# A four-layer convolution network on one core: Wu's products on four column tiles, the map's state as a square by ScalarE, layer 3's rows in the image's order

## The chip, the cores and the metric

The kernel runs on one core of a Trainium2 chip. The metric is the device time of one execution in microseconds (us), lower is better. The engines go by the short names of the profile: PE is TensorE (its matmuls), PEld its weight loads, DVE is VectorE, ACT is ScalarE, POOL is GpSimd and SP is SyncE. POOL and SP issue nearly all DMAs of this kernel, each in the order of its own queue.

## The reference

The input x holds 32 images of 8 channels by 256 by 256 pixels in float32. Four layers each add a function of the group-normalised input to their input. Layer 0 is the long one: a coupled map lattice of 15 steps, a small network with 128 hidden channels, and a gate that mixes the two.

```python
def layer0(x, K_local, Wp, bp, Wu, bu, Wg1, bg1, Wg2, bg2):
    grid = drive = x
    for _ in range(15):
        mapped = 3.9 * grid * (1.0 - grid)
        local = conv(mapped, K_local, groups=8)            # 3x3, one kernel a channel
        physics = 0.7 * mapped + 0.3 * local
        grid = 0.85 * physics + 0.15 * drive
    cml = clip(grid, 0.0001, 0.9999)
    h = relu(conv(x, Wp, bp))                              # 8 -> 128 channels, 3x3
    nca = sigmoid(conv(h, Wu, bu))                         # 128 -> 8, 1x1
    gin = concatenate([x, cml, nca], axis=1)
    g = sigmoid(conv(relu(conv(gin, Wg1, bg1)), Wg2, bg2)) # 3x3, then 1x1
    return g * cml + (1.0 - g) * nca

x = x + layer0(gn(x), ...)
x = x + layer1(gn(x), ...)   # 3x3, 8 -> 8, operands rounded to 127 levels
x = x + layer2(gn(x), ...)   # 3x3, 8 -> 8
x = x + layer3(gn(x), ...)   # 5x5 mean, one channel at a time
```

## The kernel before

The kernel has two stages. The first computes layer 0 of all images, the second layers 1 to 3.

**First stage.** Two generators are interleaved in one order that is written out by hand (the scheduler is switched off there). `lattice(b, ahead)` runs the 15 steps of image b, and `gated()`, called the rest below, runs the hidden network and the gate of image b-1. Each `yield` of the lattice hands a number to the rest: the PE time, in us, that the rest may emit before the lattice goes on. After each half-step this is `BLOCK`, 7.4. Each `yield` of the rest gives what it has used: 0.87 for a hidden product, 1.9 for a batch of Wu's products, 2.6 for three gate products. Each half-step also calls `next(ahead)`, one errand: a large DMA, or a piece of the statistics of the next image.

The lattice keeps channels 0 to 5 as patches of 16 by 8 pixels on 128 partitions, 512 patches in the free dimension, in two tiles of three channels each (half 0 and half 1, `states`). The tile holds v(v-1), so that the map and its local sum are one product. A half-step is, for each of three channels, a product inside the patch (`patch_sb`, L368) and one with the neighbours' rim (`ring_sb`, L370) into a PSUM buffer `psc`. There are three such buffers. Then DVE adds the drive (L378), forms v(v-1) in place (L384), and `spread(half)` lets SP issue four DMAs (L246) that copy the rim of the new state to `rings[half]`, for the next step's L370. Channels 6 and 7 live in `strip`, rows of the image, and are convolved by DVE with nine taps a step (L317): three taps in half 0, six in half 1. After the six, DVE clamps the sum (L395), forms v(v-1) into the strip (L396), and `edges()` lets SP issue two DMAs (L250, L251) that copy the strip's edge rows to their neighbours.

The order in half 1 is: products; L378; L384; `spread`; six taps, L395, L396; `edges`. In half 0 it is the same without L395, L396 and `edges`.

In the rest, a product of 72 rows of an im2col tile gives 128 hidden channels of two rows of pixels (`ph`, L606; three buffers), and ACT applies the rectifier (`hh`, L611). Four `hh` are a batch; Wu multiplies each into 32 columns of the PSUM tile `pn` (L582 in `second()`):

```python
for hh, r in four:
    q, i = divmod(r, 4)
    nc.tensor.matmul(pn[32 * q : 32 * q + 32, :], wu_sb[:, i, :], hh,
                     start=i == 0, stop=i == 3)
```

The rows r of a batch are (0, 4, 1, 5) or (2, 6, 3, 7), in the second half plus 8, so q changes between two values within a batch. Sixteen rows of eight channels make the 128 partitions of `pn`. The gate then reads the input (`xq`, from `nr_d`), the lattice's result (`cq`, from `cr_d`) and `nh` with the same order of partitions, 16 products (L508) with their neighbours' rows. The raw input `xc` for the residual comes from `x` by two DMAs a chunk, and DVE adds the result (L533 to L540). `x1_d` takes the image to the second stage. Statistics of an image use the `psc` buffers as well (`stats_parts`).

**Second stage.** For each image `layer1` loads `x1` (L709), rounds it in four pieces on DVE and ACT (`qh`), fetches neighbours' rows (`qb`) and multiplies (L698, L702, bf16). `layer2` does it in float32; its result `x2` goes to DRAM as `x3` in one DMA (L746), and comes back as `y`, with whole rows of the image on partitions, in 16 DMAs (L753). `layer3` normalises `y` into `xr` (L762), copies edge rows (`xr2`, L768), multiplies with a band matrix (L777, L781) and stores from SP. The program writes, in iteration b, layer 3 of image b-3, layer 2 of b-1 and layer 1 of b; there the scheduler decides the order on each engine. `x1`, `x2` and `y` have two buffers each.

Of the kernel before, what the change touches and what calls it, by code (L numbers as in the profile page):

```python
# [18 lines left out]
C = 8  # L19
# [29 lines left out]
BLOCK = 7.4  # L49
# [17 lines left out]
def kernel(  # L67
    ctx, tc, x, patch, ring, taps, pick, wp, bp, wu, bu, wg1, wga, wgb, bg1, wg2, bg2, w1, b1, w2, b2, w3,
# [24 lines left out]
    x3_d = [dram.tile([P, NPX], F32, name=f"x3_d{b}") for b in range(2)]  # L93
# [74 lines left out]
    with ExitStack() as es:  # L168
# [10 lines left out]
        taps_sb = const(wt, taps, [P, 9], "taps_sb")  # L179
        pick_sb = const(wt, pick, [P, P], "pick_sb")  # L180
# [13 lines left out]

        for t in (patch_sb, ring_sb):
            flat = t.rearrange("p c m -> p (c m)")
            nc.vector.tensor_scalar(flat, flat, -R_ * (1.0 - BETA_) * EPS_, None, ALU.mult)
# [3 lines left out]
        )  # L201
        for c in range(CP):
            nc.vector.scalar_tensor_tensor(
                patch_sb[:, c, :], eye_sb, -R_ * (1.0 - BETA_) * (1.0 - EPS_), patch_sb[:, c, :],
                ALU.mult, ALU.add,
            )
# [12 lines left out]
        for t in (*xbs, nh, zero, *hbs, *states, *rings, strip):  # L219
            nc.gpsimd.memset(t, 0.0)  # L220

        xn_d = [dram.tile([C, HP, WP], F32, name=f"xn_d{i}") for i in range(3)]
        nr_d = [dram.tile([P, HB, WP], F32, name=f"nr_d{i}") for i in range(3)]
        cr_d = [dram.tile([P, HB, WP], F32, name=f"cr_d{i}") for i in range(3)]
# [26 lines left out]
        def errands(b):  # L253
# [27 lines left out]
            if b >= 0:  # L281
                for r in four:
                    nc.gpsimd.dma_start(
                        window(
                            nr_d[b % 3], r.start * C * HB * WP,
                            [[WP, P], [C * HB * WP, 4], [1, WP]],
                        ),
                        xbs[b % 2][:, r, :],
                    )
                    yield  # L290
# [3 lines left out]
            for r in range(0, RB, 2):  # L294
                nc.vector.bn_stats(bn[:, r, :], xb[:, r, 1 : 1 + W])
                nc.vector.bn_stats(bn[:, r + 1, :], xb[:, r + 1, 1 : 1 + W])
                yield
# [9 lines left out]
        def lattice(b, ahead):  # L307
# [42 lines left out]
            for c in range(CP):  # L350
                nc.vector.scalar_tensor_tensor(
                    inner(c), dr[:, c], 1.0, dr[:, c], ALU.subtract, ALU.mult
                )
                nc.scalar.mul(dr[:, c], dr[:, c], BETA_)
                if c == 0:
                    nc.scalar.mul(d2, d2, BETA_)
                if c % HALF == HALF - 1:
                    spread(c // HALF)
                yield 1.5
            yield 4  # L360
            for step in range(STEPS):
                for half in range(2):
# [14 lines left out]
                    for c in mine:  # L377
                        nc.vector.scalar_tensor_tensor(  # L378
                            inner(c), pss[c % HALF], FLOOR, dr[:, c], ALU.max, ALU.add
                        )  # L380
                    for c in mine:
                        v = inner(c)
                        if step < STEPS - 1:
                            nc.vector.scalar_tensor_tensor(v, v, 1.0, v, ALU.subtract, ALU.mult)  # L384
                        else:
                            nc.vector.tensor_scalar(
                                dr[:, c], v, 0.0001, 1.0 - 0.0001, ALU.max, ALU.min
                            )
                    if step < STEPS - 1:
                        spread(half)  # L390
# [7 lines left out]
                    if half == 1 and step == STEPS - 1:  # L398
                        nc.vector.tensor_scalar(own, acc, 0.0001, 1.0 - 0.0001, ALU.max, ALU.min)
                    next(ahead, None)  # L400
                    yield BLOCK
# [13 lines left out]
            for r in range(0, RB, 4):  # L415
                nc.gpsimd.dma_start(
                    window(
                        cr_d[b % 3], r * C * HB * WP,
                        [[WP, HB * CP], [C * HB * WP, 4], [1, WP]],
# [5 lines left out]
            for q in range(HB // RQ):  # L425
                for c in range(2):
                    at = (C * RQ * q + CP + c) * row
                    nc.sync.dma_start(
                        window(cr_d[b % 3], at, [[WP, HB], [C * row, RQ], [1, WP]]),
# [26 lines left out]

        place = [0]

        def gated():
# [22 lines left out]
            def gate(n, quarter):  # L482
# [10 lines left out]
                for k in range(2):  # L493
                    nc.gpsimd.dma_start(
                        xc[:, k, :],
                        window(
                            x, b * C * H * W + (k0 + k) * RB * W, [[W, RB], [H * W, C], [1, W]]
                        ),
                    )
# [46 lines left out]
                for _ in stats_parts(ps_c, bn, st, gavr_sb, "psc"):  # L546
# [31 lines left out]
            def second():  # L578
                n, pn, four = late.pop()
                for hh, r in four:  # L580
                    q, i = divmod(r, 4)
# [12 lines left out]
            for n in range(B * NCH):  # L594
# [5 lines left out]
                for half in range(2):  # L600
                    im = ims.pop(0)
                    for rows in ((0, 4, 1, 5), (2, 6, 3, 7)):
                        four = []
                        for i, j in enumerate(rows):
# [11 lines left out]
                            if i == 1 and late:  # L616
                                second()
                                yield 1.9
# [8 lines left out]
            yield 1.9  # L627
# [24 lines left out]
    with ExitStack() as es:  # L652
# [80 lines left out]
        def layer2(b, x2, st):  # L733
# [12 lines left out]
            nc.gpsimd.dma_start(x3, x2)  # L746
# [5 lines left out]
            for k in range(HB):  # L752
                nc.gpsimd.dma_start(  # L753
                    y[RB * (k % 8) : RB * (k % 8) + RB, k // 8, :, :],
                    window(x3, k * W, [[C * NPX, RB], [NPX, C], [1, W]]),
# [48 lines left out]
def laid_out(inputs):  # L804
# [33 lines left out]
    def on_rows(w):  # L838
# [7 lines left out]
        return a.reshape(RB * i, 3, RB * o)  # L846
# [34 lines left out]
    for g in range(4):  # L881
# [6 lines left out]
        taps=np.tile(K[CP:, 0].reshape(2, 9), (P // 2, 1)),  # L888
        pick=np.repeat((np.arange(P) == HB * CP)[:, None], P, 1).astype(f),
# [45 lines left out]
```

## Time and profile before

| | |
|---|---|
| median of three runs | 17,328.34 us (17,284.92 to 17,337.03) |
| profiled execution, its own time | 17,311.55 us |
| its span | 17,309.7 us |
| first stage, one image in | 453 us on the mean of 31 |
| second stage | from about 14,760 us to the end |
| PE busy | 16,500.7 us, 95% of the span |
| DVE busy | 13,265.9 us, 77% |
| ACT busy | 4,089.7 us, 24% |
| POOL busy | 3,931.6 us, 23% |
| mean granted PE clock | 0.964 |

Durations in the profile come from the one profiled execution. A group of instructions is given by its line in the kernel, its engine, what it writes and reads, its shape, and its count; then follow its busy time in us, the mean of one in ns, and the idle time of the engine just before it with what ended that. A float32 product appears as two records of PE. "Windows" give the busy time of each engine in a stretch of time, in the order PE, PEld, DVE, ACT, POOL, then the granted PE clock, the busy share of the DMA engines and GB/s. A timeline line begins with the start and the duration in us.

### The profile page before, as it was taken

Reading aid. Unit: us, or ns where it says so; the run is one execution under the profiler, and the core shown is the slowest. Engines: PE = TensorE matmul, PEld = TensorE weight load, DVE = VectorE, ACT = ScalarE, POOL = GpSimd, SP = SyncE. Lnnn points to the kernel's source line nnn. Section 1 sums busy time; section 2 is a strip of 40 time slices with the busy share of each in tenths; the row PEclk is TensorE's granted clock in tenths of the full one; section 3 lists DMA queues with packets and bytes.
Section 4 is the critical chain, followed back from the end, with each engine's and each line's share of the span. In section 5 each row is a group of like instructions: output and inputs, shape, how many; then the busy total and the mean of one; then the engine's idle time right before and its main releaser. Section 6 shows DMA issues by size and latency. Waiting matters only on the chain.

```text
span 17309.7 us, 133874 instructions
## 1 busy us (share of the span) xinstructions
PE 16500.7 (95%) x42888; PEld 6670.3 (39%) x42888; DVE 13265.9 (77%) x17529; ACT 4089.7 (24%) x5982; POOL 3931.6 (23%) x6517
## 2 busy tenths in 40 slices
PE   5999999999999999999999999999999999899999
PEld 2333333333333333333333333333333333344444
DVE  8788888888888788878888887888888884555554
ACT  0222222222222222222222222222222223111110
POOL 1222222222222222222222222222222223111111
PEclk7999999999999999999999999999999999999999
DMA  3666666666666666666666666666666665455454
GB/s 82 129 129 133 133 131 134 127 132 132 133 132 131 124 133 134 128 128 128 127 134 130 129 132 129 133 133 132 133 130 131 133 127 117 113 129 125 122 131 102
DMA packets 817532, 2208.48 MB, mean 128 GB/s; under 512 B 281741, under 2 KB 485749, under 8 KB 732741
## 3 DMA queue, kind: packets, MB, share of 16 engines
q0 software_dynamic: 464384, 1425.54, 39.8%
q1 hardware_dynamic: 352452, 774.38, 21.6%
q8 instruction: 350, 5.73, 0.2%
q14 instruction: 346, 2.83, 0.1%
HBM read 1078.72 MB, written 404.28 MB: 86 GB/s over the span
## 4 chain that ended last, share of the span: by engine, by line
PE 73%; DVE 18%; DMA 5%; issue 2%; POOL 1%; SPq 1%; ACT 0%; DVEq 0%; POOLq 0%; ACTq 0%
PE ph L606 15%; PE psc L370 12%; PE psc L368 11%; DVE acc L317 10%; PE pg L508 10%; PE pn L582 8%; PE psv L777 6%; PE psv L698 5%; DMA rings<-state 3%; DVE state L384 2%; DVE state L378 2%; PE psv L702 2%; PE psv L781 1%; PE pq L519 1%; DMA im<-xn_d 1%
## 5 line engine op out<-in xcount | busy, mean ns | idle before, releaser
L317 DVE SCALAR_TENSOR_TENSOR acc<-strip,taps_sb,acc 128x1024 f32<-128x1024 f32 x3840 | 4931.3, 1284 | 120.2
L611 ACT ACTIVATE hh<-ph,bp_sb 128x512 f32<-128x512 f32 x4096 | 2812.2, 687 | 8403.9 <-PE ph L606 8338.9
L606 PE MATMUL ph<-im,wp_sb 72*128 72x512 f32 x8192 | 4042.1, 610 | 108.7 <-DMA im<-xn_d 86.6
L378 DVE SCALAR_TENSOR_TENSOR state<-psc,flat 128x512 f32<-128x512 f32 x2880 | 1894.8, 686 | 2072.5 <-PE psc L370 2009.5
L368 PE MATMUL psc<-state,patch_sb 128*128 128x512 f32 x5760 | 2762.9, 614 | 365.9 <-DVE u L112 284.4
L370 PE MATMUL psc<-rings,ring_sb 80*128 80x512 f32 x5760 | 2796.6, 623 | 81.5 <-DMA rings<-state 81.4
L476 POOL DMA_DIRECT2D im<-xn_d x3072 | 1730.5, 568 | 3501.1 <-PE ph L606 3117.7
L606 PEld LDWEIGHTS ph<-im,wp_sb 72*128 72x128 f32 x8192 | 1486.5, 191 | 2223.6 <-issue 2074.8
L582 PE MATMUL pn<-hh,wu_sb 128*32 128x512 f32 x8192 | 2022.0, 616 | 0.0
L368 PEld LDWEIGHTS psc<-state,patch_sb 128*128 128x128 f32 x5760 | 1073.6, 193 | 1921.4 <-issue 1142.3
L370 PEld LDWEIGHTS psc<-rings,ring_sb 80*128 80x128 f32 x5760 | 1138.5, 199 | 1588.6 <-issue 1550.9
L384 DVE SCALAR_TENSOR_TENSOR state<-state 128x512 f32<-128x512 f32 x2688 | 1689.7, 685 | 0.0
L777 PE MATMUL psv<-xr,w_sb 128*128 128x512 f32 x2560 | 1159.7, 595 | 0.5 <-DVE xr L762 0.5
L541 POOL DMA_DIRECT2D x_d<-xc x256 | 152.0, 594 | 4082.8 <-DVE xc L536 4017.9
L582 PEld LDWEIGHTS pn<-hh,wu_sb 128*32 128x32 f32 x8192 | 394.0, 111 | 1469.9 <-issue 1469.9
L508 PE MATMUL pg<-xq,wg_sb 128*128 128x512 f32 x1536 | 734.7, 615 | 13.0 <-DMA xq<-nr_d 13.0
L508 PE MATMUL pg<-cq,wg_sb 128*128 128x512 f32 x1536 | 735.0, 616 | 0.0
L508 PE MATMUL pg<-nh,wg_sb 128*128 128x512 f32 x1536 | 732.8, 614 | 0.0
L698 PE MATMUL psv<-xh,w_sb 128*128 128x512 f32 x1536 | 704.8, 595 | 8.1 <-DVE xh L734 4.1
L452 POOL DMA_DIRECT2D hb<-nh x576 | 320.4, 560 | 1710.4 <-ACT nh L560 1662.8
L777 PEld LDWEIGHTS psv<-xr,w_sb 128*128 128x128 f32 x2560 | 475.7, 189 | 565.9 <-issue 561.5
L786 DVE TENSOR_TENSOR y<-psv,y 128x512 f32<-128x512 f32 x256 | 176.6, 690 | 623.3 <-PE psv L781 623.0
(155 smaller groups left out, 12270.6 us busy)
## 6 DMA issues: line engine op xcount, KB each, us to landing
im<-xn_d POOLq DMA_DIRECT2D x3072, 193.3 KB, 7.3
rings<-state SPq DMA_DIRECT2D x1920, 159.5 KB
rings<-state SPq DMA_DIRECT2D x1920, 106.3 KB
strip<-strip SPq DMA_DIRECT2D x960, 126.0 KB
xn_d<-xb POOLq DMA_DIRECT2D x128, 516.0 KB, 10.3
nr_d<-xb POOLq DMA_DIRECT2D x128, 516.0 KB, 9.0
xq<-nr_d POOLq DMA_DIRECT2D x128, 516.0 KB, 11.6
cq<-cr_d POOLq DMA_DIRECT2D x128, 516.0 KB, 13.7
```

The costliest lines, as they stand in the source:

```text
L317: nc.vector.scalar_tensor_tensor(acc, strip[:, dy : dy + RQ, dx : dx + W], taps_sb[:, 3 * dy + dx : 3 * dy + dx + 1], d2 if dy == 1 and dx ...
L368: nc.tensor.matmul(pss[-1], patch_sb[:, c, :], inner(c), start=True, stop=False)
L370: nc.tensor.matmul(pss[c % HALF], ring_sb[:, c, :], rings[half][:, c % HALF, 0 : TX * SY].rearrange("p (x y) -> p x y", y=SY)[:, :, 0:TY], ...
L378: nc.vector.scalar_tensor_tensor(inner(c), pss[c % HALF], FLOOR, dr[:, c], ALU.max, ALU.add)
L384: nc.vector.scalar_tensor_tensor(v, v, 1.0, v, ALU.subtract, ALU.mult)
L476: nc.gpsimd.dma_start(im[24 * dy : 24 * dy + 24, k, 0:run], window(xn_d[b % 3], at, [[HP * WP, C], [1, 3], [1, run]]),)
L508: nc.tensor.matmul(o, wg1_sb[:, s, dx, :], src[:, :, dx : dx + W], start=s == dx == 0, stop=False,)
L582: nc.tensor.matmul(pn[32 * q : 32 * q + 32, :], wu_sb[:, i, :], hh, start=i == 0, stop=i == 3,)
L606: nc.tensor.matmul(ph.rearrange("p (k w) -> p k w", w=W), wp_sb, im[:, :, j * WP : j * WP + W], start=True, stop=True,)
L611: nc.scalar.activation(hh, ph, AF.Relu, bias=bp_sb)
L698: nc.tensor.matmul(o, w[:, dx, :], src[:, 2 * i : 2 * i + 2, dx : dx + W], start=dx == 0, stop=False,)
L777: nc.tensor.matmul(o, w3_sb[:, dx, :], xr[:, k, 2 * g : 2 * g + 2, dx : dx + W], start=dx == 0, stop=False,)
```

## The change

**Wu and the numbering of rows.** In `second()` q and i change places, and a batch takes rows (0, 1, 2, 3) or (4, 5, 6, 7), so that its four products go to four different column groups of 32. Row r of a block of 16 then stands at position (r mod 4) · 4 + r div 4. Weights are permuted to match, `nr_d` and `cr_d` are written in that order, and the raw input is written once to a new DRAM tensor `xr_d` in that order (four more errands' DMAs an image), from where `xc` comes in one DMA a chunk. The estimate for a batch in the `yield` is 1.05 instead of 1.9, and `BLOCK` is 6.5.

**The state as a square.** The tile now holds (v - 1/2)², which is v(v-1) + 1/4. The constant goes into the drive (`lift`), and the rim's border is 1/4 instead of 0. L378 writes its sum back to PSUM, and ACT forms the square from PSUM into the state. ACT also forms the first state and drive of an image.

**The order in a half-step.** It is now: products; the sum; taps, and in half 1 L395, L396 and `edges`; 1.7 us of the rest; squares; `spread`. `held` keeps the statistics of the gated image out of the PSUM buffers meanwhile.

**Layer 3's rows.** `x3_d` has the image's own order. It is written in 16 DMAs, one for each of the 16 positions, and `y` is read in two.

```diff
-BLOCK = 7.4
+BLOCK = 6.5
...
-    x3_d = [dram.tile([P, NPX], F32, name=f"x3_d{b}") for b in range(2)]
+    x3_d = [dram.tile([C, H, W], F32, name=f"x3_d{b}") for b in range(2)]
...
+        lift = wt.tile([P, CP], F32, name="lift")
+        nc.vector.tensor_reduce(lift, kern_sb, AX.X, ALU.add)
+        nc.vector.tensor_scalar(
+            lift, lift, 0.25 * R_ * (1.0 - BETA_) * EPS_, 0.25 * R_ * (1.0 - BETA_) * (1.0 - EPS_),
+            ALU.mult, ALU.add,
+        )
+        minus = wt.tile([P, 1], F32, name="minus")
+        nc.vector.memset(minus, -0.5)
...
                 nc.vector.bn_stats(bn[:, r + 1, :], xb[:, r + 1, 1 : 1 + W])
+                if r < 8:
+                    nc.gpsimd.dma_start(
+                        window(
+                            xr_d[(b + 1) % 3], r // 2 * C * HB * W,
+                            [[W, P], [4 * C * HB * W, 4], [1, W]],
+                        ),
+                        xb[:, 2 * r : 2 * r + 4, 1 : 1 + W],
+                    )
                 yield
...
             for c in range(CP):
-                nc.vector.scalar_tensor_tensor(
-                    inner(c), dr[:, c], 1.0, dr[:, c], ALU.subtract, ALU.mult
-                )
-                nc.scalar.mul(dr[:, c], dr[:, c], BETA_)
+                nc.scalar.activation(inner(c), dr[:, c], AF.Square, bias=minus)
+                nc.scalar.activation(
+                    dr[:, c], dr[:, c], AF.Identity, bias=lift[:, c : c + 1], scale=BETA_
+                )
...
                     for c in mine:
-                        nc.vector.scalar_tensor_tensor(
-                            inner(c), pss[c % HALF], FLOOR, dr[:, c], ALU.max, ALU.add
-                        )
-                    for c in mine:
-                        v = inner(c)
-                        if step < STEPS - 1:
-                            nc.vector.scalar_tensor_tensor(v, v, 1.0, v, ALU.subtract, ALU.mult)
-                        else:
+                        ps = pss[c % HALF]
+                        nc.vector.scalar_tensor_tensor(ps, ps, FLOOR, dr[:, c], ALU.max, ALU.add)
+                    if step == STEPS - 1:
+                        for c in mine:
                             nc.vector.tensor_scalar(
-                                dr[:, c], v, 0.0001, 1.0 - 0.0001, ALU.max, ALU.min
+                                dr[:, c], pss[c % HALF], 0.0001, 1.0 - 0.0001, ALU.max, ALU.min
                             )
-                    if step < STEPS - 1:
-                        spread(half)
                     for dy in (1,) if half == 0 else (0, 2):
...
                         edges()
...
+                    held.append(half)
+                    yield 1.7
+                    if step < STEPS - 1:
+                        for c in mine:
+                            nc.scalar.activation(inner(c), pss[c % HALF], AF.Square, bias=minus)
+                        spread(half)
+                    held.clear()
                     next(ahead, None)
-                    yield BLOCK
+                    yield BLOCK - 1.7
...
-                for k in range(2):
-                    nc.gpsimd.dma_start(
-                        xc[:, k, :],
-                        window(
-                            x, b * C * H * W + (k0 + k) * RB * W, [[W, RB], [H * W, C], [1, W]]
-                        ),
-                    )
+                nc.gpsimd.dma_start(xc, xr_d[b % 3][:, k0 : k0 + 2, :])
...
-                    q, i = divmod(r, 4)
+                    i, q = divmod(r, 4)
...
-                    for rows in ((0, 4, 1, 5), (2, 6, 3, 7)):
+                    for rows in ((0, 1, 2, 3), (4, 5, 6, 7)):
...
-                                yield 1.9
+                                yield 1.05
...
-            nc.gpsimd.dma_start(x3, x2)
+            for r in range(RB):
+                m = r % 4 * 4 + r // 4
+                nc.gpsimd.dma_start(
+                    window(x3, r * W, [[H * W, C], [RB * W, HB], [1, W]]),
+                    x2[C * m : C * m + C, :].rearrange("p (k w) -> p k w", w=W),
+                )
...
-            for k in range(HB):
+            for k in range(2):
                 nc.gpsimd.dma_start(
-                    y[RB * (k % 8) : RB * (k % 8) + RB, k // 8, :, :],
-                    window(x3, k * W, [[C * NPX, RB], [NPX, C], [1, W]]),
+                    y[:, k, :, :], window(x3, k * P * W, [[W, P], [H * W, C], [1, W]])
                 )
```

## The prediction

> **What bounds the kernel now.** I read the page's sums and slices first, then the groups, then the timeline of one image, then the DMA queues' waits. TensorE (PE) is busy 95% of the span, in nearly every slice.
>
> ```profile
> PE 16500.7 (95%) x42888; PEld 6670.3 (39%) x42888; DVE 13265.9 (77%) x17529; ACT 4089.7 (24%) x5982; POOL 3931.6 (23%) x6517
> ...
> PE   5999999999999999999999999999999999899999
> ```
>
> There are two stages. To about 14,760 us the lattice of image b runs beside the gated network of image b-1, one image in 453 us; then layers 1 to 3 take 2,550 us, some 78 us an image. In both PE is the bound: the windows give it 435.9 us of 453 in an image of the first stage and 499.9 of 500 in the second.
>
> ```profile
> 15500.00:16000.00 500.00, 499.85 (x1324) 222.52 (x1322) 292.37 (x582) 67.86 (x97) 77.89 (x123) 1.00 0.51 124
> 6358.00:6811.00 453.00, 435.89 (x1151) 173.70 (x1150) 371.04 (x462) 118.67 (x174) 109.84 (x185) 0.98 0.66 133
> ```
>
> The groups show what is edited: Wu's products (L582) and VectorE's (DVE's) product v(v-1) (L384).
>
> ```profile
> L582 PE MATMUL pn<-hh,wu_sb 128*32 128x512 f32 x8192 | 2022.0, 616 | 0.0
> ...
> L384 DVE SCALAR_TENSOR_TENSOR state<-state 128x512 f32<-128x512 f32 x2688 | 1689.7, 685 | 0.0
> ```
>
> In the timeline one batch of Wu's products lasts from 6002.76 to the next matmul at 6004.60: 1.84 us for eight records. They start in pairs, 6 ns apart, so two column tiles already run together.
>
> ```profile
> 6002.76 1.91 PE L582 MATMUL pn<-hh,wu_sb 128*32 128x512 f32 x8
> ...
> 6004.60 1.99 PE L606 MATMUL ph<-im,wp_sb 72*128 72x512 f32 x4
> ```
>
> The lattice is a chain beside this. For a half-step starting at 6371.75 (half 1) the ring products start at 6374.4; DVE then works through L378, L384, six taps, L395 and L396:
>
> ```profile
> 6377.88 1.89 DVE L384 SCALAR_TENSOR_TENSOR state<-state 128x512 f32<-128x512 f32 x3
> 6379.69 7.88 DVE L317 SCALAR_TENSOR_TENSOR acc<-strip,taps_sb,acc 128x1024 f32<-128x1024 f32 x6
> 6387.60 0.69 DVE L395 TENSOR_SCALAR acc<-acc 128x1024 f32<-128x1024 f32 x1
> 6388.33 1.23 DVE L396 SCALAR_TENSOR_TENSOR strip<-acc 128x1024 f32<-128x1024 f32 x1
> ```
>
> SyncE's (SP's) queue issues the ring copies (L246) right after L384, and the strip's two edge copies (L250, L251) only after L396. At L250 it stands on DVE some 8 us each time; nothing urgent is behind it.
>
> ```profile
> SPq L250 <- DVE df L533: 1050.3, 122, 13.0
> SPq L250 <- DVE bn L296: 932.1, 124, 7.6
> SPq L250 <- DVE state L378: 737.4, 104, 8.1
> ```
>
> I followed the 80 packets of 6,804 bytes of each ring copy: from its first issue to its last packet it takes 8.1 us when GpSimd's (POOL's) large copies are absent, up to 15.5 us beside them, 10.3 us on the mean. It lands a median 9.6 us (half 0) or 11.3 us (half 1) before PE wants it. So PE sets the step: two half-steps take 25.7 us outside the two places per image where a statistics product holds a PSUM buffer (PE idle 4.2 and 5.0 us, then half clock for 3.4 and 10.2 us: some 20 us an image).
>
> **What the Trainium skill says.** "TensorEngine Tiling (Array Packing)", Tiling Modes, lists 128×32 as four tiles that work in parallel, and says that a change of mode drains the engine: the trace agrees for two tiles (0.43 us a pair, 0.19 us lost round the batch). "TensorE: Matmul & The Clock Gate", Part 3, measured 3.07 times for four row tiles and says that column tiles come close; no run here shows four. "DMA: Bandwidth & Descriptors", Anatomy of one DMA: a semaphore wait happens on the issuing sequencer, not in the DMA engines; the L250 waits agree. "VectorE: DVE Perf Modes", the errata table: a ScalarE (ACT) pass of 512 out of PSUM is (172+512)/1.2 GHz = 570 ns; the trace has 687 (L611), which I use.
>
> **The change part by part.**
>
> Wu on four tiles: before, 0.10 + 1.84 = 1.94 us a batch. Four at once need two slots of 0.43 plus the same 0.19: 1.05 us (by 3.07 times, 4 × 0.856 / 3.07 = 1.12; if they do not run together, 1.94). I take 1.05: 0.89 × 32 batches = 28 us of PE an image, 910 us in all, if PE still sets the step.
>
> The square on ACT: DVE loses 84 L384 and six L351 an image at 0.685, 62 us of 371. ACT gains 90 passes at 0.687, 62 us on 119; it idles most of the time, so the work is covered. DVE's L378 now writes PSUM, which no row shows: 0.63 to 0.80 us against 0.686 (fastest and slowest PSUM-reading rows of this size, with margin); I take 0.69. The three PSUM buffers are now held until ACT's squares, which stand in ACT's in-order queue after 1.7 us of gated work: about 4.5 us after the products instead of 0.8. Behind them wait ACT's rectifiers; PE has three buffers for those, so a late DVE can stop PE for 1 to 2 us. Statistics products now also wait for the squares.
>
> The moved ring copies decide. All four copies of half 1 now follow the edge copies in SP's queue; they used to precede them. Their first issue after the ring products' start r is: L378 done at r + 3.5, six taps and L395, L396 to r + 13.3 (L384's 1.9 us is gone), two edge issues 1.65 us, so r + 15.0. Before, it was r + 5.4. The square is ready at about r + 7.5, so the wait is all the strip's. Then the copy: half 1's durations by step before were 8.1, 12.9, 11.4, 15.5, 8.7, 12.3, 9.4, 13.3, 9.4, 8.1, 14.6, 8.1, 8.4, 8.2 us, mean 10.6; the edges' 252 packets just ahead of it add some 0.7, less crossing into half 0's kinder places (mean 10.0): 10.3 + 0.7. With 0.3 us to start PE: 15.0 + 11.0 + 0.3 = 26.3 us a step. PE alone would need 25.7 - 2 × 0.9 = 23.9. So the ring's wait takes the place of Wu's 0.9 us: 14 × (26.3 - 25.7) = +8 us an image. Of the statistics stalls about half (10 us) hides in the ring's wait. ACT does the twelve first passes alone, +2. Sum: 0 us an image, between -28 (copies at 8.1 us, all of Wu's gain kept) and +15 (long copies, each wait over 3.4 us halving the clock; late DVE behind the seven gate operations of 4.8 us).
>
> Rows through xr_d: 128 POOL issues of 512 KB at 0.80 us more, 256 of xc at 0.56 fewer: -41 us on an engine busy 110 of 453. The 64 MB written are 3% more traffic, already in the upper end. Constants and the new small sums at the start: a few us. The renumbered rows themselves: 0, the same products on permuted weights.
>
> Layer 3's rows: x3 goes out in 16 issues an image instead of one, y comes in two instead of 16. Count is 18 against 17, so I would call it hidden; but the planner's order of POOL's queue changes too. Before, for each image: x3 out, y in, then x1 of three images on, a period early:
>
> ```profile
> 15983.29 0.56 POOL L746 DMA_DIRECT2D x_d<-x  x1 [55.17 <-DVE x L743]
> 15990.15 5.45 POOL L753 DMA_DIRECT2D y<-x_d  x10 [6.30 <-DMA x_d<-x]
> ...
> 16003.20 1.86 POOL L709 DMA_DIRECT2D x<-x_d  x1 [0.76 <-DMA y<-x_d]
> ```
>
> In the built program POOL's queue repeats over three images: x3(2) first row, y(1), x3(2) other rows, then x1(3), y(2), x1(4), x1(5), x3(3), x3(4) first row, y(3) and so on, while PE runs layer 2 of image 2, then layer 1 of image 3, then layer 3 of image 1. So x1(3) is asked for only when layer 2 of image 2 has ended, and PE wants it at once. In us after that end: x3's first row at 1.3; y(1), 2 MB, at the 131 GB/s of the present y copies (262 KB in 2 us) to 18; the other x3 rows at a like rate to 28 to 33; x1(3) in 7 to 13, so 36 to 44; four quantized pieces (DVE 0.80 + 0.75 + 0.68 each, ACT 1.06) 10; the neighbours' copy 4; the last products 4. Layer 1 ends at 54 to 62 instead of 7: I take 50 lost. For y(3), asked for after layer 2 of image 4 and wanted 7 us later: 18 us to land, normalising 4.4, edge copy 3 to 9, less 4.3 of products: I take 14. Ten rounds: 10 × 64 = 640 us; ends 10 × 45 and 10 × 80.
>
> **Sum.** 17,311.6 (the profiled execution; span 17,309.7) + 0 + 640 = 17,952; the median of the runs stands 17 higher: 17,970.
>
> **The rivals.** (a) Ring copies land fast and PE stays the bound in the first stage: -28.4 × 31 = -880; with layer 1's loss 17,090: faster. It decides where the copy takes under 8.6 us on the mean (15.0 + 8.6 + 0.3 = 23.9). For it: 8.1 us in seven of 14 places or close; against: POOL's copies do not go away. (b) Layers 1 to 3 lose nothing (x1 in time) and the first stage is even: 17,330. Against: PE's and POOL's orders are fixed in the program. (c) The waits add up: +15 an image, 18,440. (d) The four tiles do not run together: PE needs 25.7 again beside a chain of 26.3, and stalls hide less: +10 an image, 18,280.
>
> **How the numbers follow.** Forecast 0.50; (a) 0.13; (b) 0.06; (c) and (d) 0.31. About 0.3% is what a measurement of this kernel can tell from no change. Faster 0.15 (a, a part of b), same 0.04, slower 0.81. The range leaves out the deep end of (a) and of (c): 17,250 to 18,450.
>
> **What would show it.** Wu's batch at 1.05 us; PE waiting on the ring copies in half 1, several us; SP's L265 waiting on DVE, the copies behind it; PE under 90% busy in both stages; POOL's x3 copies waiting, then PE idle some 50 us every third image. Wrong if PE stays above 95% in either stage, or an image takes under 435 us.

## The result, and the profile after

| | before | after |
|---|---|---|
| median | 17,328.15 us | 19,224.97 us |
| runs | 17,284.92 to 17,337.03 (4) | 19,200.07 to 19,257.56 (4) |
| first stage, to layer 1's first product | 14,780 us | 15,939 us |
| second stage, from there to the last product's end | 2,524 us | 3,253 us |
| one image of the first stage, mean of 29 | 453.1 us | 488.8 us |

The ratio is 1.110, 95% interval 1.108 to 1.113: the change makes the kernel 11.0% slower. The forecast was 3.7% slower, 17,970 us, and the result lies above its range. Of the 1,888 us between the two profiled spans, 1,160 came in the first stage, where I had put nothing, and 729 in the second, where I had put 640.

The page of the changed kernel, its sums, then the slices of PE and of the granted clock: PE falls to 7 and 8 tenths only in the last seven slices, the second stage, while its clock is at 7 or 8 tenths in the first 32.

```profile
PE 17131.2 (89%) x42888; PEld 6886.5 (36%) x42888; DVE 11684.7 (61%) x14652; ACT 5772.1 (30%) x8862; POOL 3928.5 (20%) x6421
...
PE   5899999999999999999999999999999997787878
...
PEclk7888888888888888888888888888888898898989
```

Windows of the changed kernel, one image of the first stage and 500 us of the second (columns as for the kernel before). Before, PE stood still for 17 of 453 us and had clock 0.98; now for 40 of 489, at 0.88. In the second stage it had no idle time at clock 1.00, and now 103 us of 500.

```profile
6358.00:6847.00 489.00, 448.50 (x1129) 177.24 (x1128) 318.61 (x370) 170.43 (x263) 109.15 (x181) 0.88 0.59 125
16400.00:16900.00 500.00, 396.59 (x999) 173.28 (x998) 223.25 (x425) 51.27 (x71) 59.17 (x91) 0.88 0.41 98
```

The groups of the changed kernel: the edit of the operations did what it should. DVE's sum into PSUM (L402) takes 697 ns, the square is ACT's (L421), Wu's group (L606) is down from 2,022 us. But the ring products (L393) waited 688 us on their copies, against 81 us before (L370).

```profile
L402 DVE SCALAR_TENSOR_TENSOR psc<-psc,flat 128x512 f32<-128x512 f32 x2880 | 1957.5, 697 | 5140.3 <-PE psc L393 5131.2
...
L393 PE MATMUL psc<-rings,ring_sb 80*128 80x512 f32 x5760 | 3055.4, 671 | 819.6 <-DMA rings<-state 687.8
...
L421 ACT ACTIVATE state<-psc,minus 128x512 f32<-128x512 f32 x2688 | 1697.9, 689 | 2678.6 <-DVE psc L402 2661.9
...
L606 PE MATMUL pn<-hh,wu_sb 128*32 128x512 f32 x8192 | 1257.6, 687 | 0.0
```

**One wait, step by step.** The timeline of PE in the changed kernel, around a step of half 1. Counts are records, two for each product. Wu's batch runs from 6444.47 to the next product at 6445.47: 1.00 us, so four tiles do run together. The ring products start at 6452.44, those of the next step at 6482.00, after 7.33 us of waiting for the copy.

```profile
6444.47 1.06 PE L606 MATMUL pn<-hh,wu_sb 128*32 128x512 f32 x8
6445.47 1.99 PE L630 MATMUL ph<-im,wp_sb 72*128 72x512 f32 x4
...
6452.44 2.74 PE L393 MATMUL psc<-rings,ring_sb 80*128 80x512 f32 x6
...
6482.00 3.75 PE L393 MATMUL psc<-rings,ring_sb 80*128 80x512 f32 x4 [7.33 <-DMA rings<-state]
```

The same stretch on SP's queue: the edges go out at 6465.79, once DVE's L413 is done, and half 1's four ring copies only from 6467.58, 15.1 us after their step's start, though ACT had their squares ready by 6456.7. Half 0's four follow at once, in the same line of eight.

```profile
6465.79 0.83 SPq L265 DMA_DIRECT2D strip<-strip  x1
6466.66 0.80 SPq L266 DMA_DIRECT2D strip<-strip  x1
6467.58 13.35 SPq L261 DMA_DIRECT2D rings<-state  x8
```

**The clock after it.** PE's timeline goes on without a hole, and every product takes twice its time, up to 6504 or so: 5.46 us for six records of ring products that took 2.74, 3.62 for four of hidden products that took 1.88. Only when six records of full height come in a row (L391, 128 rows) does the speed return: L393 is back at 2.74.

```profile
6482.00 5.46 PE L393 MATMUL psc<-rings,ring_sb 80*128 80x512 f32 x6 [7.33 <-DMA rings<-state]
6487.26 1.92 PE L630 MATMUL ph<-im,wp_sb 72*128 72x512 f32 x2
6488.96 1.91 PE L532 MATMUL pg<-ha,wga_sb 96*128 96x512 f32 x2
6490.67 1.91 PE L533 MATMUL pg<-hb,wgb_sb 72*128 72x512 f32 x2
6492.38 3.62 PE L630 MATMUL ph<-im,wp_sb 72*128 72x512 f32 x4
6495.93 1.94 PE L606 MATMUL pn<-hh,wu_sb 128*32 128x512 f32 x8
6497.79 3.78 PE L630 MATMUL ph<-im,wp_sb 72*128 72x512 f32 x4
6501.37 4.20 PE L391 MATMUL psc<-state,patch_sb 128*128 128x512 f32 x6
6505.40 2.74 PE L393 MATMUL psc<-rings,ring_sb 80*128 80x512 f32 x6
```

The Trainium skill, "TensorE: Matmul & The Clock Gate", Part 1, says that the full clock comes after at least one busy window of about 3.4 us. Here PE is busy for over 20 us before it does, so busy time alone is not what counts. The mean spell at half clock lasts 14.9 us (206 of them from 1,000 to 13,500 us of the span); before, 7.2 us (115): there are more spells, and the mean one is twice as long.

**What brings the clock back.** The traces of before, after, a1, c1, c2, e1 and f1 (below) show it. Every change of the clock in them falls on a grid of 3.41 us. I took each such window of the first stage, from 1,000 to 13,500 us, and weighted PE's time in it by the rows of its products (rows of zeros counted in), as a share of 128. Of the 3,230 windows at half clock, none of the 1,736 with a share under 0.74 was followed by full clock, and all of the 895 with 0.86 or more were; the 599 between them went either way. At full clock, all 994 windows under 0.40 were followed by half clock, and none of the 20,714 with 0.55 or more. Busy time alone does not sort them: in the changed kernel PE was busy through 810 windows at half clock, and after 606 of these the clock stayed at half. In the stretch above, the window from 6494.07 to 6497.48 holds hidden products and most of a batch of Wu, 98 of 128 rows on the mean (0.76), and the clock stays at half; the one from 6500.90 to 6504.31, mostly L391, has 120 rows (0.94), and full clock follows.

**The sum of an image.** From the records of PE and of the clock, the mean of 29 images (the first two and the last left out). "Cold" is time in which PE works at half clock; half of it is lost. (The expectations below count all time at half clock, 118 us in the changed kernel, of which PE works in 111.5.) The work at full speed is what is left of the image after the idle time and half the cold time.

| kernel | image | PE idle | cold | work at full speed |
|---|---|---|---|---|
| before | 453.1 | 16.8 | 26.8 | 423.0 |
| after | 488.8 | 36.4 | 111.5 | 396.6 |
| a1_spread_first | 446.2 | 22.8 | 54.2 | 396.3 |
| c1_full_rows | 464.8 | 50.1 | 33.2 | 398.1 |
| e1_two_tiles | 467.5 | 21.6 | 44.1 | 423.8 |
| f1_block | 487.4 | 43.4 | 95.3 | 396.4 |
| c2_before_full | 444.9 | 17.0 | 10.1 | 422.9 |
| a9_best_block | 441.6 | 35.1 | 21.0 | 396.0 |
| a10_sp | 427.5 | 22.9 | 16.2 | 396.4 |

The last column is a check on this way of counting: it takes two values only, 423 with Wu on two column tiles and 396 to 398 on four. So the change took 26.4 us of work from an image, and added 19.6 of idle time and 42.3 by the clock: +35.5.

**The second stage.** POOL's timeline in the changed kernel, from the end of layer 2 of an image: first row of x3, then y of the image before, then the other rows of x3 (the last at 17,079), and only then layer 1's x1 (L733).

```profile
17059.51 0.59 POOL L772 DMA_DIRECT2D x_d<-x  x1 [75.10 <-DVE x L767]
17060.30 1.84 POOL L782 DMA_DIRECT2D y<-x_d  x2 [0.20 <-issue]
17062.13 3.58 POOL L772 DMA_DIRECT2D x_d<-x  x6
...
17079.11 0.59 POOL L772 DMA_DIRECT2D x_d<-x  x1 [0.34 <-DMA x_d<-x]
17081.71 0.58 POOL L733 DMA_DIRECT2D x<-x_d  x1 [2.01 <-DMA x_d<-x]
```

And PE in the same stretch: it waits 33.73 us for the first rounded piece, which x1 holds up, and 8.03 us for the neighbours' copy.

```profile
17098.33 5.54 PE L722 MATMUL psv<-qh,w_bf 128*128 128x512 bf16 x15 [33.73 <-ACT qh L702]
17111.90 2.31 PE L726 MATMUL psv<-qb,w_bf 72*128 72x512 bf16 x5 [8.03 <-DMA qb<-qh]
```

### The profile page after: what moved, and what is told of

Same layout as the page of the kernel before. It is cut to its first block, busy times and chain, and to the rows that moved or that the text cites. A ratio compares the mean times of both kernels' runs of the same rounds, so it can differ in the third digit from the quotient of the medians.

```text
span 19198.3 us, 136492 instructions
## 1 busy us (share of the span) xinstructions
PE 17131.2 (89%) x42888; PEld 6886.5 (36%) x42888; DVE 11684.7 (61%) x14652; ACT 5772.1 (30%) x8862; POOL 3928.5 (20%) x6421
## 5 line engine op out<-in xcount | busy, mean ns | idle before, releaser
L402 DVE SCALAR_TENSOR_TENSOR psc<-psc,flat 128x512 f32<-128x512 f32 x2880 | 1957.5, 697 | 5140.3 <-PE psc L393 5131.2
L630 PE MATMUL ph<-im,wp_sb 72*128 72x512 f32 x8192 | 4661.8, 690 | 232.8 <-DMA im<-xn_d 119.3
L393 PE MATMUL psc<-rings,ring_sb 80*128 80x512 f32 x5760 | 3055.4, 671 | 819.6 <-DMA rings<-state 687.8
L391 PE MATMUL psc<-state,patch_sb 128*128 128x512 f32 x5760 | 2879.7, 637 | 174.8 <-DVE u L112 86.1
L630 PEld LDWEIGHTS ph<-im,wp_sb 72*128 72x128 f32 x8192 | 1663.5, 215 | 2737.3 <-issue 2164.7
L421 ACT ACTIVATE state<-psc,minus 128x512 f32<-128x512 f32 x2688 | 1697.9, 689 | 2678.6 <-DVE psc L402 2661.9
L393 PEld LDWEIGHTS psc<-rings,ring_sb 80*128 80x128 f32 x5760 | 1184.5, 210 | 2466.7 <-issue 2461.6
L391 PEld LDWEIGHTS psc<-state,patch_sb 128*128 128x128 f32 x5760 | 1139.2, 203 | 1860.5 <-issue 1390.2
L606 PE MATMUL pn<-hh,wu_sb 128*32 128x512 f32 x8192 | 1257.6, 687 | 0.0
L772 POOL DMA_DIRECT2D x_d<-x x512 | 318.8, 632 | 2357.6 <-DVE x L767 2108.8
L527 PE MATMUL pg<-cq,wg_sb 128*128 128x512 f32 x1536 | 785.4, 652 | 0.0
```

The lines of the kernel that those rows point to most:

```text
L391: nc.tensor.matmul(pss[-1], patch_sb[:, c, :], inner(c), start=True, stop=False)
L393: nc.tensor.matmul(pss[c % HALF], ring_sb[:, c, :], rings[half][:, c % HALF, 0 : TX * SY].rearrange("p (x y) -> p x y", y=SY)[:, :, 0:TY], ...
L402: nc.vector.scalar_tensor_tensor(ps, ps, FLOOR, dr[:, c], ALU.max, ALU.add)
L421: nc.scalar.activation(inner(c), pss[c % HALF], AF.Square, bias=minus)
L527: nc.tensor.matmul(o, wg1_sb[:, s, dx, :], src[:, :, dx : dx + W], start=s == dx == 0, stop=False,)
L630: nc.tensor.matmul(ph.rearrange("p (k w) -> p k w", w=W), wp_sb, im[:, :, j * WP : j * WP + W], start=True, stop=True,)
```

## The experiments

Every ratio is to the kernel before on the same chip. Labels that begin with a, e and f, and c1, start from the changed kernel; b4 and c2 start from the kernel before.

**The place of the ring copies: a1_spread_first.** Half 1's edges are issued after its ring copies.

```diff
-                        edges()
...
                         spread(half)
+                        if half == 1:
+                            edges()
```

> One part of the change undone: the strip's two edge copies are issued after half 1's ring copies again, everything else as in the changed kernel (19,225 us). Theory A, the ring copies behind the edges make PE wait and let its clock fall: PE's idle time ahead of the ring products falls from 24 us an image to under 5, the half clock from 118 us an image to 30 to 60, the image from 489 us to 425 to 440, so 17,100 to 17,750 us in all; layers 1 to 3 stay as slow as they are. Rival B, the squares on ACT and the PSUM buffers held for them are what slows the lattice: the image stays over 470 us, over 18,600 us in all. Rival C, PE's clock falls because Wu's products on four tiles leave too little activity: half clock stays near 118 us an image though the waits go, 18,200 to 18,700 us.

17,772.29 us, ratio 1.026 (1.024 to 1.028): 1,453 us back, all in the first stage. PE's group of ring products in this kernel waits for copies as little as before:

```profile
L393 PE MATMUL psc<-rings,ring_sb 80*128 80x512 f32 x5760 | 2816.8, 627 | 125.7 <-DMA rings<-state 76.4 <-issue 30.4 <-DMA strip<-strip 18.8
```

So the order in SP's queue makes the waits: idle time falls by 13.6 us an image and cold time by 57. With that order alone put back, the image is 7 us under that of before. The total lies just over its range, and the image is 446 us, not 425 to 440; the cold time that is left, 54 us, is twice that of before. Rival B is out.

**Layer 3's copies: a2_rows_back and a3_both.** x3 keeps the layout of before; because of the new row numbers it is written by four DMAs of 32 partitions, and y is read by 16 again. a3 is this together with a1's edit.

```diff
-            for r in range(RB):
...
+            for j in range(4):
+                nc.gpsimd.dma_start(
+                    window(x3, j * C * NPX, [[4 * C * NPX, 4], [NPX, C], [1, NPX]]),
+                    x2[32 * j : 32 * j + 32, :],
+                )
```

> Layer 3's rows as before, as far as the new numbering allows: x3 goes out in four DMAs of 32 partitions and y comes in 16, and with them the order in which POOL's queue holds the x1 loads comes back to one a period ahead. The first stage is as in the changed kernel. Theory D, the late x1 and y are what layers 1 to 3 lose: that stage falls from 3,259 us to 2,520 to 2,560, so 18,470 to 18,560 us in all. Rival E, the second stage is slow for the DMAs' own traffic in short rows, not the order: little comes back, 18,900 us or more.

> Both undone together: edge copies after half 1's ring copies, and layer 3's rows as before; Wu on four tiles, the square on ACT and the renumbered rows stay. Theories A and D add up: 16,400 to 17,000 us, faster than both kernels, with PE over 94% busy in the first stage. If Rival B or C holds, 17,500 us or more.

a2: 18,946.78 us, ratio 1.094 (1.092 to 1.096). a3: 17,461.99 us, 1.009 (1.006 to 1.012). Only 292 and 283 us of the 729 came back: the second stage took 2,961 and 2,970 us, against 2,524 before. Both missed: theory D had the second stage back at 2,520 to 2,560 us. What still kept it long was open.

**Rows in use and the clock: c1_full_rows and c2_before_full.** The 72-row and 80-row products get 128 rows; the added weights are zero, and `im_all` are two tiles of 128 rows, zeroed once. c1 does it to the changed kernel, c2 to the kernel before.

```diff
-        rings = [wt.tile([RING, HALF, SN], F32, name=f"rings{i}") for i in range(2)]
+        rings = [wt.tile([P, HALF, SN], F32, name=f"rings{i}") for i in range(2)]
...
-                im = imp.tile([72, 2, 8 * WP], F32, name="im")
+                im = im_all[half]
```

> The changed kernel, with the products of 72 rows (the hidden ones) and of 80 rows (the ring's) taken over all 128 rows: the added rows of weights are zero, those of the moving tile zero or 1/4, so nothing else changes and each product streams the same 512 columns. The trace of the changed kernel shows the clock staying at half for a median of 13.7 us once it has fallen (6.8 before the change), through windows filled with these products and with Wu's, and rising after windows with products of 128 rows. Theory F, rows in use count for the clock: half clock falls from 118 us an image to under 70, the image from 489 us to 450 to 470, 18,000 to 18,700 us in all. Rival G, the clock goes by PE's idle time alone, or zero rows count for nothing: 19,150 to 19,300 us, half clock as it was.

> The kernel before, unchanged but for its 72-row products of the input (Wp) and 80-row products of the ring, which are padded to 128 rows with zero weights: the same number of products of the same length. Theory F (the clock follows the rows in use as well as the time in use): half-clock time in the first stage falls from 29.8 us per image to 8 to 20 us, worth 5 to 11 us per image, total 16,950 to 17,200 us. Theory G (only holes in the product stream count): 29.8 us stay, total 17,280 to 17,370 us. A loss (17,400 us or more) would mean that the padding costs TensorE or DMA time in itself.

c1: 18,467.43 us, ratio 1.066 (1.064 to 1.068). PE is idle for longer, 50.1 us an image, yet cold for 33 instead of 111: with as many holes and more, the clock came back sooner. c2: 17,058.83 us, 0.985 (0.982 to 0.987), cold time 10 instead of 27. So rows in use count for the clock, in either kernel, and the zero rows cost at most 1.5 us of work an image.

**Tiles or block: e1_two_tiles and f1_block.** f1 changes `BLOCK` alone, the first pair of lines below; e1 also puts Wu back on two tiles, with its `yield` of 1.9.

```diff
-BLOCK = 6.5
+BLOCK = 7.4
...
-                    for rows in ((0, 1, 2, 3), (4, 5, 6, 7)):
+                    for rows in ((0, 1, 4, 5), (2, 3, 6, 7)):
```

> The changed kernel with Wu's products on two column tiles again (row numbering, square, spread order and layer 3 as changed; the budget of a block back at 7.4 and Wu's share at 1.9). It puts back some 0.85 us of TensorE work per batch, 28 us per image, outside the lattice as before. Theory P (the Wu saving was real and merely buried under the ring waits; the clock does not care how Wu is tiled): 28 us x 31 images come on top, half-clock time stays at 105 to 130 us per image, total 19,950 to 20,150 us. Theory T (with four tiles the clock stays low longer because a window of Wu and 72-row products no longer holds enough work in the array; two tiles let it come back): half-clock time per image falls from 118 to 50 to 85 us and gives back 15 to 30 us per image, total 19,150 to 19,600 us. Theory A (only the ring chain counts, TensorE work is hidden in its waits): TensorE idle per image falls from 36 to below 15 us, total 19,200 to 19,350 us. The second stage stays at 3,260 us in all three.

> The changed kernel with one number put back: the budget of other TensorE work in a block, 7.4 as before instead of 6.5; Wu stays on four tiles. The run with two tiles had both put back and gained 697 us although it does 28 us more TensorE work per image. Theory K (that gain was the block's: with 0.9 us less cover per half the ring copies arrive too late, waits come and the clock falls): TensorE idle falls from 36 to 18 to 25 us per image and half-clock time from 118 to 40 to 65 us as with two tiles, but without their 28 us, total 17,600 to 18,000 us. Theory T (it was the tiles: two tiles keep more work in the array and the clock comes back sooner): idle 30 us or more, half-clock time 95 us or more, total 18,900 to 19,300 us. Between them both count. The second stage stays at 3,260 us.

e1: 18,528.54 us, ratio 1.069 (1.066 to 1.072), quicker than the changed kernel although it does 27 us more work an image, and quicker than any of its theories had it (19,150 us at the least). f1: 19,157.32 us, 1.106 (1.102 to 1.109), as its theory T. The windows of ten images each show it, the changed kernel, then e1, then f1, each line from its own kernel (second number PE busy, then the clock third from the end):

```profile
6436.65:11324.16 4887.51, 4529.92 (x11382) 1793.70 (x11381) 3195.30 (x3710) 1703.20 (x2630) 1096.26 (x1811) 0.88 0.59 125
```

```profile
6166.03:10820.38 4654.35, 4455.70 (x11381) 1751.62 (x11380) 3203.86 (x3710) 1711.60 (x2630) 1093.45 (x1810) 0.95 0.61 132
```

```profile
6398.97:11277.11 4878.14, 4445.00 (x11381) 1781.66 (x11380) 3202.35 (x3710) 1699.99 (x2630) 1092.06 (x1810) 0.88 0.59 126
```

The longer block halves the waits on ring copies (from 23.9 to 12.5 us an image) and yet leaves clock 0.88; the two tiles bring 0.95. But the pair does not differ in the tiles' effect on the clock alone: with four tiles the longer block runs the rest dry, so that PE's idle time as a whole is 43.4 us in f1 against 21.6 in e1, and there are 9.3 spells at half clock an image against 5.8. The spells are shorter too, 7.9 us against 12.0.

Their length follows from the windows. At half clock a batch of Wu takes 1.87 us on four tiles and 3.56 us on two (medians). A window that holds a whole batch on four tiles, and hidden products else, has by these medians (1.87 × 128 + 1.54 × 72) / 3.41 = 103 of 128 rows, a share of 0.80, in the range that goes either way; on two tiles the batch alone is longer than a window. So four tiles save PE's time and take full-height work out of the stretch in which the clock could recover.

**What was left in the second stage: b4_writes.** One line of the kernel before: four writes of x3 in place of one.

```diff
-            nc.gpsimd.dma_start(x3, x2)
+            for j in range(4):
+                nc.gpsimd.dma_start(x3[32 * j : 32 * j + 32, :], x2[32 * j : 32 * j + 32, :])
```

> The kernel before, unchanged but for one line of layer 2: x3 is written by four DMAs of 32 partitions instead of one of 128, the same bytes to the same places. Theory R (the rest of the second stage's loss lies in GpSimd's order: with four writes the planner puts the next image's x1 load ahead of y's sixteen reads, y lands later, and layer 3's first products wait): the second stage grows from 2,524 us to 2,930 to 3,000 us as in the changed kernel with the rows' copies put back, the first stage stays, total 17,720 to 17,830 us. Rival (four writes are as good as one, and what is left comes from the rows numbered anew): 17,290 to 17,380 us.

17,790.29 us, ratio 1.026 (1.024 to 1.028), second stage 2,984 us: the number of writes makes the whole rest of a2 and a3. POOL's timeline in this kernel shows the order that the planner now makes, x1's load (L709) ahead of y's reads and behind a wait of 9.85 us for its buffer:

```profile
16538.85 1.98 POOL L747 DMA_DIRECT2D x_d<-x  x4 [60.40 <-DVE x L743]
16550.68 0.56 POOL L709 DMA_DIRECT2D x<-x_d  x1 [9.85 <-DVE x L727]
16551.41 4.98 POOL L754 DMA_DIRECT2D y<-x_d  x7 [0.17 <-issue]
```

y's last read is issued 33 us after x3's first write on the mean; in the kernel before, where x1's load comes after y, 19 us. That this order on POOL is what costs the time is not shown, for the planner's order changed on other engines as well. DVE first normalises y (L763) a median of 82 us after x3's first write, although y has landed after 44; before, 34 and 27. And PE, idle for 308 us of this stage (before, 42; the clock costs another 178), waits mainly for DVE's statistics (L101, 88 us; L108, 65) and for the edge copies of `xr` (102), not for y itself.

**Putting it together: a6_best, a8_best, a9_best_block, a10_sp.** a6 is a3 with full rows and with x1 loaded by SP. a8 is a6 with layers 1 to 3 on the row order of before: x1 is loaded in four quarters, by POOL, x3 written in one DMA, and the weights of layers 1 and 2 are not permuted. a9 is a8 with `BLOCK` 7.4. a10 is a8 with the quarters issued by SP, as the lines below have it.

```diff
-            nc.gpsimd.dma_start(x1, x1_d[b])
+            for j in range(4):
+                nc.sync.dma_start(
+                    x1[32 * j : 32 * j + 32, :],
+                    window(x1_d[b], j * C * NPX, [[4 * C * NPX, 4], [NPX, C], [1, NPX]]),
+                )
```

> The kernel with half 1's ring copies ahead of the edge copies and layer 3's rows in four writes and sixteen reads, with two things more: the 72-row and 80-row products padded to 128 rows with zero weights, and layer 1's load of x1 issued by SyncE instead of GpSimd, so that no load of x1 stands ahead of y's reads on GpSimd's queue. Theory R (what was left of the second stage's loss, 437 us, is y's reads waiting behind x1's load): the second stage falls from 2,976 us to 2,520 to 2,650 us. Theory S (it is the order that the planner gives TensorE and VectorE around layer 3): it stays at 2,850 us or more. First stage: theory F of the clock, half-clock time 55 us per image to 20 to 35 us, image 445.6 to 428 to 437 us; if rows don't count there, 445. Totals: F and R 16,500 to 16,850 us, under the kernel before; F and S 16,900 to 17,200 us.

> The fastest kernel so far with layers 1 to 3 on the rows in the order of before: x1's load puts the rows back in order (four loads of 32 partitions on GpSimd in place of one), and x3 is written by one DMA as before. First stage as there, 426.8 us per image. Theory R (the second stage's loss is the planner's order of GpSimd's copies: y behind x1): x3 is ahead of y again with at most one quarter of x1 between them, the second stage falls from 2,710 us to 2,520 to 2,590 us, total 16,430 to 16,520 us. Theory Q (more and smaller copies of one queue cost in themselves, wherever they stand): 2,650 us or more, total 16,560 us or more.

> The same kernel as the one with layers 1 to 3 on the rows of before, and the block's budget 7.4 instead of 6.5. If the ring copies still come late at 6.5 with their new place ahead of the edges (waits on them are only 2.7 us per image there), 7.4 brings at most 3 us per image: total 16,340 to 16,500 us, like its twin or up to 0.5% faster. If cover beyond the need only delays the lattice (blocks last 0.9 us longer and the work left for between the images doesn't shrink by as much), up to 4 us per image more: up to 16,650 us.

> The kernel with layers 1 to 3 on the rows of before (x1's load in four quarters), these quarters issued by SyncE instead of GpSimd: GpSimd has only x3's write and y's reads, as early as before, and the quarters are spread over the image between SyncE's small copies. Theory R: the second stage falls from 2,838 us (quarters on GpSimd, the last one behind y's reads) to 2,520 to 2,620 us, total 16,480 to 16,590 us. Rival (the quarters behind SyncE's edge copies come late as well, or hold these up): 2,710 us or more, 16,670 us or more.

| kernel | median | ratio | second stage |
|---|---|---|---|
| a6_best | 16,619.34 us | 0.959 (0.957 to 0.961) | 2,710 us |
| a8_best | 16,804.94 us | 0.969 (0.968 to 0.971) | 2,838 us |
| a9_best_block | 17,259.66 us | 0.995 (0.994 to 0.997) | 2,844 us |
| a10_sp | 16,494.11 us | 0.951 (0.950 to 0.953) | 2,546 us |

a6 got its first stage and missed the second. x1's load is gone from POOL's queue, and yet y's first read is issued 12.8 us after x3's first write, as in b4 (12.6; before, 7.3): with four writes y is late wherever x1's load stands. Still the second stage is 260 us shorter than in a3; the planner's orders changed again, and which of them brought this is open. a8 missed too: in 29 of 32 images a quarter of x1 stands between x3's write and y's first read, and PE waits 182 us in all for layer 1's neighbours (10 us of it at 15,338). Its time lies in its rival's range; neither run tells whether the number of copies in one queue has a cost of its own. a9 lies far over its range: the longer block ran the rest dry, and PE waits 10.0 us an image for the transposes' input and 8.5 for `xq`, where a8 has 0.8 and 2.6. In a10, which differs from a8 only in the queue of the quarters, POOL's timeline is that of the kernel before again, y straight behind x3:

```profile
15547.32 0.57 POOL L777 DMA_DIRECT2D x_d<-x  x1 [58.51 <-DVE x L774]
15554.20 6.05 POOL L784 DMA_DIRECT2D y<-x_d  x11 [6.31 <-DMA x_d<-x]
```

a10 beats both kernels, by 4.9% and by 14%: it keeps the four tiles, the square and `xr_d`, and loses neither the copies' places nor the clock.

## Why the prediction was wrong

- **Sign and places: right, but for one sign.** Slower, ring copies behind the edges, x1 behind x3: all seen. PE under 90% came in the second stage alone (79% in the window shown). In an image of the first stage PE is busy for 452 of 488.8 us, 93%: what it loses there is mostly the clock, not idle time.
- **Wu on four tiles: right.** A batch was put at 1.05 us and took 1.00; an image was to lose 28 us of work and lost 26.4. Rival (d) is out.
- **The square and DVE's sum: right.** 689 and 697 ns against 687 and 690. The statistics stalls hid as supposed: before the patch products PE waited 9.2 us an image for them and now 2.8.
- **The ring chain: the path was right, its sum 2 us short.** From half 1's step to the next a median of 28.8 us passed, where 26.3 was put (26.4 before). The first issue came a median of 15.2 us after the step's start, as put, and the copies took 9.6 us on the mean, 11.0 put; but from the last packet to a waiting PE it took a median of 2.0 us, not 0.3. PE waited for the copy in 164 of 406 steps; in the others it came to these products later than the copy. That PE's idle time grew by 19.6 us, where 14 × 2.4 - 10 = 24 was put, is luck in part: fewer waits, but longer ones. Rival (a) leaned on seven copies of 14 near 8.1 us; its list has six.
- **The step that failed is "Sum: 0 us an image, between -28 ... and +15".** It counted the waits as time and left their effect on the clock to the upper end. The clock cost 42.3 us an image, 31 × 42 = 1,310 us, more than the whole excess of 1,255 us over the forecast. The upper end and rival (c) had the waits halve the clock, at +15 an image in all; it was +35.5. The term that was mis-sized is the spell at half clock after a wait. I had 3.4 and 10.2 us for it, from the kernel before. The mean spell got twice as long, 14.9 us instead of 7.2, and there were 206 in place of 115. They were long because few rows were at work after a wait: filling up the rows cut the mean spell to 5.5 us (c1). The same edit had taken Wu's full-height time out of that stretch, which the windows show; e1 against f1 agrees, but has fewer waits as well.
- **Layer 3's rows: right in mechanism, a little small.** 640 us put, 729 measured, within 450 to 800. In the whole stage PE waited 428 us for layer 1's pieces and neighbours and 149 for layer 3's input, 43 and 15 a round where 50 and 14 were put; the clock, put at nothing here, cost 98, and other waits the rest. That POOL's count of copies says little was right as well; that even four writes instead of one change the planner's orders, and cost 460 us (b4), I had not looked for.

## What to carry to other kernels

Price a wait of TensorE as its length plus half of the spell at half clock after it, and look at what stands in the queue just then: products with few rows lengthen the spell, and so does a change that makes full-height ones shorter. Zero rows that fill short products up to the full height can then be the cheapest gain of all (c2: 1.5% of the kernel before, for no other change). When a planner orders the queues, compare its orders on every engine before and after for any change in the number of DMAs; moving one load to another queue brought back 292 us of the second stage (a10 against a8).

## What the hardware showed that was not expected

The granted clock follows how many rows of the array work, not only whether it works: PE ran 22 us without a hole at half clock on products of 72 to 96 rows with one batch of Wu among them (6482 to 6504), and the same products with zero rows added cut the cold time from 111 to 33 us an image in one kernel and from 27 to 10 in another. In windows of 3.41 us the limit for coming back lies between 0.74 and 0.86 of the rows, and the limit for falling between 0.40 and 0.55.

Columns do not count in the same way. On two column tiles Wu's products fill half of the array's columns; yet with a limit of 0.75 the rows alone misplace 7 of the 241 windows at half clock of the kernel before, and rows times columns at best 41. Four column tiles at work together did not make up for their shorter time either: a batch of Wu in 1.00 us holds the rows for a shorter time than the same batch in 1.84 us, and the clock comes back later.
